# Row-tiled G matrices, a new split of the PSUM banks and a new order in a fused convolution and state-space kernel

## The chip, the cores and the metric

The kernel runs on one core of a Trainium2 chip. A core has five engines that work side by side, each through its own queue in order: TensorE (PE in the profile, its weight loads are PEld), VectorE (DVE), ScalarE (ACT), GpSimd (POOL) and SyncE (SP), which here issues the DMA transfers. The metric is the device time of one execution in microseconds. Three runs of the kernel before took 2834.29, 2833.24 and 2831.9 us, with a median of 2833.24 us. The profiled execution, from which all durations below come, took 2833.51 us and its trace spans 2831.8 us.

## What is computed

The input is 128 images of 128 channels and 16x16 pixels in float32. Layer 0 is a pair of quantised 3x3 convolutions with batch normalisation. Layer 1 reads each image as 256 tokens of 128 channels, runs a state-space mixer over the tokens forward and backward, and then a router with eight experts. The mixer is where the change lies. Cut to what matters, for each direction:

```
z, xbc, dt = split(x @ in_proj)
xbc  = silu(causal_conv4(xbc));  xh, B, C = split(xbc)     # 4 heads of 64; B and C have 64 rows
dt   = softplus(dt + dt_bias);   a = cumsum(dt * A)
L    = exp(a[l] - a[s]) for s <= l, else 0                 # per head
y[l] = sum_s (C[l] . B[s]) * L[l, s] * dt[s] * xh[s] + D * xh[l]
out  = rmsnorm(y * silu(z)) @ out_proj
```

The reference computes the sum over s in chunks of 64 tokens with a carried state. The kernel computes the same sum over an image's 256 tokens at once, in blocks of 128 by 128. The products C[l] . B[s] are the G matrices: one for each image and direction, with a contraction over only 64 rows.

## The kernel before

The first part of the kernel (up to about 297 us) is layer 0: statistics, the first convolution, the second. Layer 1 follows as a software pipeline over 64 steps. Step i handles two images (index k), that is 512 tokens, in two directions (index d). Its work is cut into parts, and each part is a Python generator whose pieces end at a `yield`:

- `a`: load, transpose, first layer norm. `c`: the dt chain, once for two steps, with small DVE pieces, and DMA transfers that bring the log decays into `rows` and `cols`.
- `x` (L747): input projections for xh, B and C: one matmul, one ACT pass and three DVE passes that read the PSUM bank (L762, L768). `bc` (L774): silu over B and C, and two DMA transfers that move C to the partitions where B lies. `sx`, `z`, `xt`: silu of xh, the gate z, the transpose of xh.
- `g` (L816): the G matrices, into PSUM. `s` (L828): exponents, bf16 matmuls, and the ACT exponential that empties the bank (L846). `m` (L849): DVE multiplies the exponentials by G (L852, L857) and so holds G's bank until then.
- `y` (L862): y = xh^T times the products. Here heads q=0 and q=1 use 64 output columns each, so two matmuls address two column halves of the array. `n`, `r`, `o`: norm and output projection.
- `e`, `p`, `f`: second layer norm, router, gates (with a DMA round trip through DRAM), GpSimd scaling (L1020), and the eight expert matmuls accumulated in one bank `f_ps` (L1032), which is copied out at L1035.

What sets the order is the table `T`. It gives each piece of each part a time in units of the pipeline's period. Piece n of step i gets the key i + T, all keys are sorted, and the pieces are issued in that order. So `T` fixes the order in every engine's queue, and nothing else: no instruction waits for its time, only for its operands and buffers.

In `part_g` before, one call handles one direction and one image. The stationary operand is the whole tile `bc` of that direction (128 partitions: B in one half, C in the other). The moving operand `cc` holds C in the rows that face B, and zeros in the other half. The zeros are written once, by four memsets at L584, ahead of the pipeline. The contraction so runs over 128 rows, of which 64 count.

PSUM has eight banks, which `BANKS` hands out by tag: x (projections, z, exponents) three, y two, f one, o (everything else, G too) two.

Of the kernel before, what the change touches and what calls it, by code (L numbers as in the profile page):

```python
# [8 lines left out]
F32 = mybir.dt.float32  # L9
# [5 lines left out]
P = 128  # L15
NT = 256
# [4 lines left out]
HD = 64  # L21
# [10 lines left out]
def kernel(ctx: ExitStack, tc: tile.TileContext, a: dict):  # L32
    from concourse import bass_isa

    nc = tc.nc
# [259 lines left out]
    with tc.tile_pool(name="w1p", bufs=1) as w1p:  # L295
# [15 lines left out]
        with tc.tile_pool(name="setup1", bufs=1) as setup, tc.tile_pool(  # L311
            name="psa", bufs=1, space=PSUM
# [8 lines left out]
            for i in range(NP):  # L321
                t = res.tile([P, 2, NT], F32, name=f"xr{i}", tag=f"xr{i}")
# [37 lines left out]
            for c in range(4):  # L360
                of = slice(cuts[c], cuts[c + 1])
# [33 lines left out]
                n = cuts[c + 1] - cuts[c]  # L395
# [145 lines left out]
    late = ctx.enter_context(tc.tile_pool(name="late", bufs=1))  # L541
# [34 lines left out]
                        )  # L576


    cczs = [[late.tile([P, 2 * NT], F32, name=f"cc{k}_{d}") for d in range(2)] for k in range(2)]
    gts = [late.tile([P, P], F32, name=f"gt{k}") for k in range(2)]  # L580
    daz = late.tile([P, 2, P], F32, name="daz")
    lwz = late.tile([P, P], F32, name="lwz")
    for t in (*cczs[0], *cczs[1], *gts, daz, lwz):
        nc.gpsimd.memset(t, 0.0)  # L584
    pr = ctx.enter_context(tc.tile_pool(name="pr", bufs=2))
    sm = ctx.enter_context(tc.tile_pool(name="sm", bufs=2))
    ps_ = ctx.enter_context(tc.tile_pool(name="ps", bufs=1, space=PSUM))
    BANKS = {"x": 3, "y": 2, "f": 1, "o": 2}

    def bank(name, tag):  # L590
        return ps_.tile([P, 512], F32, name=name, tag=tag, bufs=BANKS[tag])

# [8 lines left out]
    yts, uTs, xcs, xts, bcs, ccs, zs = {}, {}, {}, {}, {}, {}, {}  # L601
    gps, es, ygs, sqs, rrs, t2s, u2Ts, fps, gbs = {}, {}, {}, {}, {}, {}, {}, {}, {}
# [171 lines left out]
    def part_bc(i):  # L774

        bc = bcs[i]
        nc.scalar.activation(bc, bc, AF.Silu)
        yield

        cc = ccs[i] = cczs[i % 2]  # L780
        nc.sync.dma_start(cc[0][0:64, :], bc[64:128, 0, :])
        nc.sync.dma_start(cc[1][64:128, :], bc[0:64, 1, :])
        yield

    def part_sx(i, d):
# [27 lines left out]

    def part_g(i, d, k):  # L816

        tok = lambda s: slice(k * NT + s * P, k * NT + (s + 1) * P)
        g_ps = gps[i, d, k] = bank(f"g_ps{i}_{d}_{k}", "o")
        nc.tensor.matmul(  # L820
            g_ps[:, 0:NT], bcs[i][:, d, tok(d)], ccs[i][d][:, k * NT : (k + 1) * NT], start=True, stop=True
        )
        nc.tensor.matmul(  # L823
            g_ps[:, NT : NT + P], bcs[i][:, d, tok(1 - d)], ccs[i][d][:, tok(1 - d)], start=True, stop=True
        )
        yield

    def part_s(i, d, k, j):  # L828
# [193 lines left out]

    def part_f(i):

        f_ps = bank(f"f_ps{i}", "f")
        for t in range(4):
            nc.tensor.matmul(
                f_ps[:, t * P : (t + 1) * P], t2s[i][:, t, :], ident, start=(t == 0), stop=False, is_transpose=True
            )
        yield  # L1030
        for e in range(NE):
            nc.tensor.matmul(f_ps, ew[:, e, :], gbs[i, e], start=False, stop=(e == NE - 1))  # L1032
            yield
        ob = pr.tile([P, 2, NT], F32, name=f"ob{i}", tag="ob", bufs=1)
        nc.scalar.copy(ob.rearrange("p b s -> p (b s)"), f_ps)  # L1035
        yield
        nc.sync.dma_start(out_c[:, 2 * i : 2 * i + 2, :], ob)
        yield

    def part_t(i):  # L1040
# [4 lines left out]


    T = {
        ("a",): [0.0773, 0.0895, 0.1152, 0.2866, 0.3447, 0.4794, 0.4953, 0.5115],
        ("c",): [
            1.4709, 1.5225, 1.5731, 1.6594, 1.7098, 1.7751, 1.7801, 1.8040, 1.8079, 1.8309, 1.8542, 1.8594,  # L1050
            1.9139, 1.9270, 1.9323, 1.9709, 2.0549, 2.2383, 2.3648, 2.4555, 2.5636, 2.5771, 2.8047, 2.9326,
            2.9591, 3.1958, 3.3130, 3.3131, 4.1355, 4.1893,
        ],
        ("t",): [3.6635],
        ("x", 0, 2): [2.4693, 2.5057, 2.5934, 2.5972, 2.5984],
        ("x", 0, 0): [2.1661, 2.2763, 2.4457, 2.4862, 2.5014],
        ("x", 0, 1): [2.6018, 2.6937, 2.7181, 2.7588, 2.8003],
        ("x", 1, 2): [2.8997, 2.9367, 2.9373, 3.0152, 3.0293],
        ("x", 1, 0): [2.9802, 3.0015, 3.1146, 3.1362, 3.1518],
        ("x", 1, 1): [3.2863, 3.3092, 3.3641, 3.3704, 3.3905],  # L1060
        ("bc",): [3.4178, 3.4667],
        ("sx", 0): [2.9714],
        ("sx", 1): [3.5025],
        ("z", 0, 0): [3.2114, 3.2933],
        ("z", 0, 1): [3.4975, 3.5653],
        ("z", 1, 0): [3.3125, 3.4208],
        ("z", 1, 1): [3.5685, 3.5821],
        ("xt", 0, 0): [3.0438, 3.0552],
        ("xt", 0, 1): [3.3605, 3.4527],
        ("xt", 1, 0): [3.6676, 3.7471],  # L1070
        ("xt", 1, 1): [3.8466, 3.8846],
        ("g", 0, 0): [3.7660],
        ("s", 0, 0, 0): [3.6873, 3.7772],
        ("s", 0, 0, 1): [3.7508, 3.7854],
        ("s", 0, 0, 2): [3.8420, 3.8432],
        ("m", 0, 0): [3.8517, 3.8548],
        ("g", 0, 1): [3.9427],
        ("s", 0, 1, 0): [3.5860, 3.6728],
        ("s", 0, 1, 1): [3.8506, 3.9139],
        ("s", 0, 1, 2): [3.7919, 3.8284],  # L1080
        ("m", 0, 1): [3.9845, 3.9955],
        ("g", 1, 0): [4.0723],
        ("s", 1, 0, 0): [3.9718, 4.0401],
        ("s", 1, 0, 1): [4.0786, 4.1032],
        ("s", 1, 0, 2): [4.0576, 4.0790],
        ("m", 1, 0): [4.2309, 4.2498],
        ("g", 1, 1): [4.2898],
        ("s", 1, 1, 0): [3.6494, 3.7294],
        ("s", 1, 1, 1): [4.1026, 4.2262],
        ("s", 1, 1, 2): [3.9153, 3.9444],  # L1090
        ("m", 1, 1): [4.3058, 4.3095],
        ("y", 0, 0): [4.0126, 4.2204, 4.3180, 4.4089],
        ("y", 0, 1): [4.0291, 4.1343, 4.2948, 4.4250],
        ("y", 1, 0): [4.4415, 4.7048, 4.7862, 4.8156],
        ("y", 1, 1): [4.4007, 4.5565, 4.7642, 4.7846],
        ("n", 0): [4.7414, 4.7578, 4.8130],
        ("n", 1): [4.8600, 4.9321, 4.9637],
        ("r",): [4.9642],
        ("o", 0): [4.9857, 5.0427],
        ("o", 1): [4.9997, 5.0508],  # L1100
        ("e",): [
            5.0510, 5.2202, 5.2252, 5.2390, 5.2794, 5.2900, 5.3284, 5.3630, 5.3646, 5.3758, 5.3781, 5.3951,
            5.4117, 5.4132, 5.4233, 5.4552, 5.4561, 5.4691, 5.4826, 5.4906, 5.5973, 5.5985, 5.6126, 5.6739,
            5.6949, 5.6950, 5.7124, 5.7406, 5.7729,
        ],
        ("p", 0): [5.7845, 6.0128, 6.1273],
        ("p", 1): [6.0774, 6.1446, 6.2610],
        ("p", 2): [6.1581, 6.2483, 6.4846],
        ("f",): [6.0920, 6.1605, 6.2981, 6.5482, 6.5709, 6.6493, 6.7506, 6.8279, 6.9171, 7.0523, 7.5749],
        ("p", 3): [6.4896, 6.7491, 6.8564],  # L1110
    }
    parts = {
        "a": part_a, "c": part_c, "x": part_x, "bc": part_bc, "sx": part_sx, "z": part_z, "xt": part_xt, "g": part_g,
        "s": part_s, "m": part_m, "y": part_y, "n": part_n, "r": part_r, "o": part_o, "e": part_e, "p": part_p,
        "f": part_f, "t": part_t,
    }
    steps = []
# [41 lines left out]
```

## Time and profile before

| what | value |
|---|---|
| median of three runs | 2833.24 us |
| span of the trace | 2831.8 us |
| layer 0, up to the last convolution | about 297 us |
| two steady steps (1509.25 to 1585.85 us) | 76.60 us, so 38.30 us a step |
| PE busy in these 76.60 us | 76.31 us |
| DVE, ACT, POOL busy in them | 66.41, 62.82, 45.97 us |
| function table loads on ACT in them | 9, of 1283 ns each |
| granted PE clock in them | 1.00 |

The profile's page gives, in this order, the busy time of each engine, the same in 40 slices of the span, the DMA queues, the chain of work that ended last, and the costliest groups of instructions by source line. A float32 matmul stands in the trace as two instructions, a bf16 matmul or a transpose as one. [...]what a matmul costs in a stream is the distance from its start to the next one's start. The chain of waits shows these distances.

### The profile page before, as it was taken

The numbers are of one execution on the slowest core, as the hardware profiler recorded it, in microseconds if no ns is written. First come the engines' busy times: TensorE is split into PE (matmuls) and PEld (weight loads), VectorE is DVE, ScalarE is ACT, GpSimd is POOL, SyncE is SP. The second block draws the span as 40 slices with busy tenths as digits, with TensorE's granted clock in tenths as the row PEclk, the third lists the DMA queues.
The fourth block names the chain that finished last, engine by engine and source line by source line (L and its number), as shares of the span: only waits on it lengthen the run. The fifth ranks groups of instructions, "written<-read, shape, count | busy, mean of one in ns | idle before, by whom it ended". The sixth has DMA issues, their size and how long they took to land.

```text
span 2831.8 us, 48012 instructions
## 1 busy us (share of the span) xinstructions
PE 2640.0 (93%) x15830; PEld 1765.6 (62%) x15830; DVE 2387.6 (84%) x6315; ACT 2219.2 (78%) x3747; POOL 1592.5 (56%) x1619
## 2 busy tenths in 40 slices
PE   0687499999999999999999999999999999999997
PEld 0232256666667666666666666666666666666664
DVE  7799688888888888888888888888888888888883
ACT  5687498888888888888888888888888888888771
POOL 1353325656565665566565556556566666555666
PEclk9899799999999999999999999999999999999998
DMA  8259212232223233222223222322232222232232
GB/s 265 86 209 318 83 30 81 83 92 89 72 81 92 76 92 91 90 68 88 87 81 91 89 80 73 92 77 91 92 90 70 85 91 77 92 90 82 67 91 97
DMA packets 164553, 273.99 MB, mean 97 GB/s; under 512 B 46144, under 2 KB 89152, under 8 KB 164288
## 3 DMA queue, kind: packets, MB, share of 16 engines
q1 hardware_dynamic: 164288, 270.75, 31.0%
q8 instruction: 131, 2.15, 0.3%
q14 instruction: 134, 1.10, 0.1%
HBM read 196.66 MB, written 57.25 MB: 90 GB/s over the span
## 4 chain that ended last, share of the span: by engine, by line
PE 79%; ACT 9%; DVE 4%; issue 2%; DMA 1%; POOL 1%; SPq 0%; POOLq 0%; DVEq 0%; ACTq 0%
PE f_ps L1032 14%; PE x_ps L750 10%; PE y_ps L871 8%; PE o_ps L920 8%; PE z_ps L793 7%; PE xt_ps L805 4%; PE n_ps L900 4%; PE y_ps L877 4%; PE sg L836 4%; PE g_ps L820 3%; PE rt_ps L949 2%; PE dt_ps L660 2%; ACT u L621 2%; PE g_ps L823 1%; PE sg L838 1%
## 5 line engine op out<-in xcount | busy, mean ns | idle before, releaser
L1020 POOL TENSOR_TENSOR gb<-gb,u2T 128x512 f32<-128x512 f32 x512 | 645.6, 1277 | 9.6 <-DMA gb<-gd 8.6
L768 DVE SCALAR_TENSOR_TENSOR xc<-x_ps,cw,xc 128x510 f32<-128x510 f32 (+2 forms) x768 | 570.4, 743 | 60.0 <-ACT xc L762 51.6
L1032 PE MATMUL f_ps<-gb,ew 128*128 128x512 f32 x1024 | 526.3, 597 | 5.0 <-POOL gb L1020 4.8
L846 ACT ACTIVATE e<-sg 128x512 f32<-128x512 f32 x768 | 455.2, 594 | 49.9 <-PE sg L836 43.2
L887 POOL TENSOR_TENSOR yg<-yg,z 128x512 f32<-128x512 f32 x256 | 324.3, 1279 | 167.1 <-DVE yg L883 143.2
L852 DVE TENSOR_TENSOR e<-e,g_ps 128x1024 f32<-128x1024 f32 x256 | 311.9, 1218 | 113.9 <-PE g_ps L823 111.2
L750 PE MATMUL x_ps<-uT,wx 128*128 128x512 f32 x768 | 398.9, 601 | 2.9 <-ACT z L797 1.4
L809 ACT COPY xt<-xt_ps 128x512 f32<-128x512 f32 x256 | 149.2, 583 | 232.3 <-PE xt_ps L805 232.3
L871 PE MATMUL y_ps<-e,xt 128*64 128x256 f32 x2048 | 314.5, 385 | 0.3 <-DVE e L852 0.3
L768 DVE SCALAR_TENSOR_TENSOR bc<-x_ps,cw,bc 128x510 f32<-128x510 f32 (+2 forms) x384 | 284.7, 741 | 24.3 <-ACT bc L762 19.7
L793 PE MATMUL z_ps<-uT,wz 128*128 128x512 f32 x512 | 265.7, 602 | 2.0 <-ACT z L797 2.0
L920 PEld LDWEIGHTS o_ps<-wo,yg 128*128 128x128 f32 x2048 | 238.7, 192 | 29.9 <-issue 29.1
L990 POOL TENSOR_TENSOR e<-euler,e 128x4 f32<-128x4 f32 x64 | 66.1, 1032 | 335.3 <-DVE e L988 335.3
L1032 PEld LDWEIGHTS f_ps<-gb,ew 128*128 128x128 f32 x1024 | 176.2, 192 | 107.3 <-issue 86.5
L920 PE MATMUL o_ps<-wo,yg 128*128 128x128 f32 x2048 | 239.2, 275 | 0.1
L910 POOL TENSOR_TENSOR rr<-rr,mhalf 128x8 f32<-128x8 f32 x64 | 105.3, 1645 | 214.6 <-DVE rr L904 214.6
L896 POOL TENSOR_TENSOR sq<-sq,sq 128x512 f32<-128x512 f32 x128 | 163.3, 1276 | 109.3 <-ACT sq L890 109.2
L173 PE MATMUL cv<-hpad,wq 128*128 128x512 bf16 x640 | 164.1, 403 | 57.1 <-DVE hpad L165 54.1
L797 ACT ACTIVATE z<-z_ps 128x512 f32<-128x512 f32 x256 | 152.6, 597 | 81.2 <-PE z_ps L793 79.1
L762 ACT ACTIVATE xc<-x_ps,cb,cw 128x512 f32<-128x512 f32 x256 | 198.0, 773 | 13.3 <-PE x_ps L750 9.1
L877 PE MATMUL y_ps<-e,xt 128*64 128x128 f32 x2048 | 198.9, 273 | 0.0
L836 PE MATMUL sg<-rows,cols 128*128 128x256 bf16 x1024 | 195.3, 273 | 1.0 <-ACT e L846 0.8
(247 smaller groups left out, 5712.8 us busy)
## 6 DMA issues: line engine op xcount, KB each, us to landing
gb<-gd SPq DMA_DIRECT2D x256, 512.0 KB
xr<-in_x SPq DMA_DIRECT2D x64, 256.0 KB
y<-xr SPq DMA_DIRECT2D x64, 256.0 KB
y<-y SPq DMA_DIRECT2D x64, 256.0 KB
cc<-bc SPq DMA_DIRECT2D x128, 128.0 KB
out<-ob SPq DMA_DIRECT2D x64, 256.0 KB
o<-o SPq DMA_DIRECT2D x56, 256.0 KB
q<-o SPq DMA_DIRECT2D x56, 256.0 KB
```

Source lines behind the costliest of these rows:

```text
L750: nc.tensor.matmul(ps, wx[d][:, n * P : (n + 1) * P], uTs[i], start=True, stop=True)
L768: nc.vector.scalar_tensor_tensor(acc[:, :, to], raw[:, :, of], cw[:, d, n, 3 - back : 4 - back], acc[:, :, to], ALU.mult, ALU.add,)
L793: nc.tensor.matmul(ps, wz[:, d, n * P : (n + 1) * P], uTs[i], start=True, stop=True)
L836: nc.tensor.matmul(sg[:, :, of], c_[:, k, d, s, half, :], r_[:, :, d, t, of], start=True, stop=True)
L846: nc.scalar.activation(e0[:, :, t, :] if j < 2 else e1, sg, AF.Exp)
L852: nc.vector.tensor_tensor(e0.rearrange("p h t l -> p h (t l)"), e0.rearrange("p h t l -> p h (t l)"), gps[i, d, k][:, 0:NT].unsqueeze(1).t ...
L871: nc.tensor.matmul(y_ps[64 * q : 64 * q + 64, k, :], xt[:, 2 * k + s0, 64 * h : 64 * h + 64], e0[:, h].rearrange("p t l -> p (t l)"), star ...
L877: nc.tensor.matmul(y_ps[64 * q : 64 * q + 64, k, s1 * P : (s1 + 1) * P], xt[:, 2 * k + s1, 64 * h : 64 * h + 64], e1[:, h, :], start=False ...
L887: nc.gpsimd.tensor_tensor(yg, yg, zs[i, d][:, n, :], ALU.mult)
L920: nc.tensor.matmul(o_ps[:, (2 * j + d) * P : (2 * j + d + 1) * P], ygs[i, d, n][:, t * P : (t + 1) * P], wo[d][:, n, :], start=(n == 0), s ...
L1020: nc.gpsimd.tensor_tensor(gb[:, e], gb[:, e], u2Ts[i], ALU.mult)
L1032: nc.tensor.matmul(f_ps, ew[:, e, :], gbs[i, e], start=False, stop=(e == NE - 1))
```

## The change

Four things change.

1. `cc` becomes one tile from a rotating pool. Forward C goes to partitions 0 to 63, backward C to partitions 64 to 127. There is no zero half, and the four memsets go.
2. `part_g` now handles both directions of one image. Each matmul contracts over 64 rows only. Forward uses the upper 64 rows of the array and backward the lower 64, in adjacent pairs: first the two 128x256 blocks, then the two 128x128 blocks. The two directions write two different banks.
3. `BANKS`: x has two banks instead of three, y keeps two but also serves `f_ps`, and o has four instead of two.
4. `T` is replaced as a whole. Each part keeps its pieces; their order in each queue changes.

```
-    cczs = [[late.tile([P, 2 * NT], F32, name=f"cc{k}_{d}") for d in range(2)] for k in range(2)]
...
-    for t in (*cczs[0], *cczs[1], *gts, daz, lwz):
+    for t in (*gts, daz, lwz):
         nc.gpsimd.memset(t, 0.0)
...
-    BANKS = {"x": 3, "y": 2, "f": 1, "o": 2}
+    BANKS = {"x": 2, "y": 2, "o": 4}
...
-        cc = ccs[i] = cczs[i % 2]
-        nc.sync.dma_start(cc[0][0:64, :], bc[64:128, 0, :])
-        nc.sync.dma_start(cc[1][64:128, :], bc[0:64, 1, :])
+        cc = ccs[i] = pr.tile([P, 2 * NT], F32, name=f"cc{i}", tag="cc")
+        nc.sync.dma_start(cc[0:64, :], bc[64:128, 0, :])
+        nc.sync.dma_start(cc[64:128, :], bc[0:64, 1, :])
...
-    def part_g(i, d, k):
+    def part_g(i, k):
+        g_ps = [bank(f"g_ps{i}_{d}_{k}", "o") for d in range(2)]
         tok = lambda s: slice(k * NT + s * P, k * NT + (s + 1) * P)
-        g_ps = gps[i, d, k] = bank(f"g_ps{i}_{d}_{k}", "o")
-        nc.tensor.matmul(
-            g_ps[:, 0:NT], bcs[i][:, d, tok(d)], ccs[i][d][:, k * NT : (k + 1) * NT], start=True, stop=True
-        )
-        nc.tensor.matmul(
-            g_ps[:, NT : NT + P], bcs[i][:, d, tok(1 - d)], ccs[i][d][:, tok(1 - d)], start=True, stop=True
-        )
+        for s, to, of in ((0, slice(0, NT), slice(k * NT, (k + 1) * NT)), (1, slice(NT, NT + P), None)):
+            for d in range(2):
+                rows_ = slice(HD * d, HD * d + HD)
+                t = tok(d) if s == 0 else tok(1 - d)
+                nc.tensor.matmul(
+                    g_ps[d][:, to], bcs[i][rows_, d, t], ccs[i][rows_, t if of is None else of], start=True, stop=True
+                )
...
-        f_ps = bank(f"f_ps{i}", "f")
+        f_ps = bank(f"f_ps{i}", "y")
...
-        ("g", 0, 0): [3.7660],
-        ("s", 0, 0, 0): [3.6873, 3.7772],
+        ("g", 0): [4.8439],
+        ("s", 0, 0, 0): [4.7381, 4.7593],
...
-        ("y", 1, 0): [4.4415, 4.7048, 4.7862, 4.8156],
-        ("y", 1, 1): [4.4007, 4.5565, 4.7642, 4.7846],
+        ("y", 1, 0): [5.4960, 5.5576, 5.7044, 5.8186],
+        ("y", 1, 1): [5.3862, 5.4334, 5.7041, 5.8037],
...
-        ("f",): [6.0920, 6.1605, 6.2981, 6.5482, 6.5709, 6.6493, 6.7506, 6.8279, 6.9171, 7.0523, 7.5749],
+        ("f",): [7.3274, 7.3434, 7.4166, 7.7003, 7.8571, 7.9726, 8.0377, 8.1134, 8.1688, 8.1967, 8.3291],
```

## The prediction, made before the changed kernel had run

> **What bounds the kernel now.** I read the page first: the busy shares of the engines and the same in slices.
>
> ```profile
> PE 2640.0 (93%) x15830; PEld 1765.6 (62%) x15830; DVE 2387.6 (84%) x6315; ACT 2219.2 (78%) x3747; POOL 1592.5 (56%) x1619
> ...
> PE   0687499999999999999999999999999999999997
> ```
>
> From slice 6 to the last but one PE is never below 90%. Then I cut two steady steps out of the middle, at the starts of two output projections, and asked for the busy time of each half.
>
> ```profile
> 1509.25:1547.50 38.25, 37.96 (x233) 25.91 (x233) 32.62 (x87) 31.79 (x52) 22.81 (x23) 1.00 0.27 82
> 1547.50:1585.85 38.35, 38.35 (x244) 26.93 (x243) 33.79 (x92) 31.04 (x53) 23.16 (x23) 1.00 0.28 85
> ```
>
> The columns are window, length, then busy time of PE, PEld, DVE, ACT, POOL. PE fills the 38.30 us of a step; DVE needs 33.2, ACT 31.4, POOL 23.0. So a step costs what PE's queue costs, and the other engines count only where PE waits for them. The chain of waits in these windows shows what each piece costs on PE, start to start:
>
> ```profile
> 1512.82 0.58 PE y_ps L871 x4
> 1513.40 0.22 PE y_ps L877 x4
> 1513.62 0.43 PE y_ps L871 x4
> ...
> 1515.57 0.60 PE xt_ps L805 x4
> ...
> 1520.40 1.28 ACT L698
> ...
> 1522.62 0.49 ACT u2T L945
> 1523.11 0.04 issue
> 1523.16 1.16 PE rt_ps L949 x8
> ...
> 1537.77 0.44 PE xt_ps L805 x4
> ...
> 1540.50 0.43 PE g_ps L820 x2
> 1540.94 0.22 PE g_ps L823 x2
> ```
>
> The reader is to see three things. One float32 matmul of 256 columns (two instructions) costs 0.43 us in G. In y, two of them (x4) cost the same 0.43 us, so the two column halves run at once. The first group of a y visit costs 0.58 instead of 0.43 us, and the transposes after it 0.60 instead of 0.44: entering and leaving the tiled mode costs 0.15 + 0.16 = 0.31 us. And once in two steps the chain leaves PE for 7 us of ACT work with a table load of 1.28 us (L698) in it.
>
> **What the Trainium skill says.** "TensorEngine Tiling (Array Packing)", Key Properties: changing the tiling mode drains TensorE; the tiles load weights and multiply independently. The trace agrees for column halves (0.31 us a visit, two matmuls in the time of one); it has no row tiles. The same page, Gotcha 1: different row tiles must write different PSUM banks, as the change has it. "TensorE: Matmul & The Clock Gate", Measured speedup vs the span model: four row tiles gave 3.07x, three column tiles 2.38x, about 77 to 79% of the ideal; y here reaches all of its 2x. "ScalarE: Activation LUTs", What ACT_TABLE_LOAD costs: about 1283 ns and a drain of about 1380 ns; the trace shows 1283 ns and the next ACT instruction at once, so I use 1.28 us.
>
> **The change part by part**, per step, on PE.
>
> G. Before: 4 calls x (0.43 + 0.22) = 2.60 us. After: 2 calls, each two pairs. With y's overlap a pair costs one matmul, so 2 x 0.65 = 1.30: a saving of 1.30 us. Bounds: 0 (no overlap) and 1.30. If only the weight loads went one after the other, a 128x256 pair would stay at 0.43 and a 128x128 pair cost 0.43 (four loads of 0.11), so 2 x 0.86 = 1.72 and a saving of 0.88. I take 1.30: y's two halves start within 0.01 us of each other, weight loads included.
>
> Mode changes. Before there are two y visits a step, each with both heads' calls (n = 0 and 1) side by side. In the new order y(0,1) and y(0,0) stand side by side, but y(1,1) and y(1,0) are parted by f, z and x matmuls, because f now holds one of the two y banks over 0.87 of a period (keys 7.3274 to 8.1968). So there are three y visits and two G visits: 3 more, 3 x 0.31 = +0.93 us.
>
> ACT's table loads. In ACT's order the changed kernel has 129 in the pipeline against 286: the Silu pieces now stand together, and so do the exponentials. (286 - 129) x 1.283 / 64 = 3.1 us a step less, so ACT falls from 31.4 to 28.3 us. ACT is not the bound; what counts is PE's wait. In the two steps above the half with the r matmuls (1.06 + 0.44 = 1.50 us) has 0.29 us less of PE work than the half with the dt matmuls (2 x 0.89), yet from one output projection to the next it takes 1547.67 - 1509.25 = 38.42 against 38.18 us. The stall is 0.53 us in two steps, 0.26 a step. The load at L698 is in its chain and goes: -0.26. Bounds: 0 and -0.36, which adds the small delays of the z and x matmuls.
>
> Banks. With two x banks an exponent matmul waits for the exponential two places ahead. A handover costs 0.16 (a sg matmul shows 0.38 but its successor starts after 0.22) + 0.59 (L846) + two semaphores of some 0.03 = 0.81 us. The PE work in between, in the new order: before s(0,0,2) one x, 0.86; before s(1,1,0) two transposes, 0.88; before s(1,1,2) gt and f, 0.97; before x(1,2) n and s, 1.11. In the old order the shortest was 1.08. Before s(0,0,2) ACT also does exponential, transpose copy, exponential: 0.16 + 0.59 + 0.58 + 0.59 + 0.09 = 2.01 us against 1.97 of PE work. So these places are just met or missed by hundredths: +0.10 us, bounds 0 and 1.25 (five places late by 0.25 each). DVE's banks have more room: x(0,1) to s(0,0,1) has 4.14 us of PE work against 0.16 + 0.77 + 3 x 0.74 + 0.1 = 3.25. The single y bank is free 0.16 + 0.74 after y(1,1); x, f and z, 2.58 us, stand in between. G holds its o banks until m, for which there are now four.
>
> DMA. `cc` still takes two transfers of 128 KB. On SP they stand behind the fourth gb load, which waits for f's second expert (key 7.4166). That is 0.43 of a period, some 16 us, before G, and the longest late transfer on the chain took 3.98 us. Other transfers move with their parts and keep over 5 us. I cost these at nothing: PE's own queue hides them.
>
> Sum per step: -1.30 + 0.93 - 0.26 + 0.10 = -0.53 us. PE is the bound from about 385 to 2766 us, 62 steps: -33 us.
>
> The start. Four memsets go from the head of POOL's queue:
>
> ```profile
> 298.90 8.42 POOL L584 MEMSET cc<- 128x512 f32 x4 [64.28 <-DMA parts<-none]
> ...
> 306.78 2.15 DVE L565 CAST cols<-triple 128x3072 bf16<-128x3072 f32 x1
> ...
> 309.74 8.67 POOL L572 TENSOR_SCALAR_AFFINE_SELECT cols<-far 64x256 bf16<-64x256 bf16 x24
> 318.38 1.02 POOL L616 TENSOR_TENSOR rstda<-rstda,mhalf 128x4 f32<-128x4 f32 x1
> ```
>
> The first layer norm's power on POOL at 318.38 is on the chain, and everything on POOL ahead of it stands in a row. Without the 8.42 us the selects start earlier, but the last third of them needs DVE's cast that ends at 308.93: 308.93 + 8.67/3 = 311.8. So 318.4 - 311.8 = -6.6 us.
>
> Fill and drain. From the first x to the last piece the keys span 7.57 - 2.17 = 5.41 periods before and 8.33 - 3.34 = 4.99 after; the prefetch that makes the pipeline look longer is only an earlier load. The tail after the last output projection (2794.4 to the end, 37 us) is the same chain of router, DMA and experts. The fill loses one or two table loads from its chain: -1 us, between -5 and +4.
>
> Together -33 - 6.6 - 1 = -40.6 us. The profiled span, 2831.8, lies 1.4 below the median of the three runs, which agree within 0.1%; I put the difference on the median: 2833.2 - 40.6 = about 2793 us.
>
> **The rivals.**
> - Weight loads in series: saving 0.88 instead of 1.30, 0.42 x 62 = 26 us less, so 2819. For it: 128 weight columns for each row tile against 64 in y, and 77% in the skill's four-tile figure. Against it: the two row tiles' loads fill different rows, and together no more of the array than one full load.
> - No overlap, the change doing only harm on PE: +1.30 x 62 = 81, so 2873. Against it: y.
> - Slower by the x banks: all five tight handovers late by 0.25 us. Price 1.25 instead of 0.10, so 2793 + 71 = 2864. It decides from 0.10 + 40.6/62 = 0.75 us a step, 0.15 at each place. For it: ACT's queue is in order, and one late copy delays the exponentials behind it. Against it: ACT now idles a quarter of the step, so a delay is caught up before the next group.
> - Better: G visits drain for half the price and no handover misses: -0.10 - 0.30 = -0.40 x 62 = -25, so 2768.
>
> **How the numbers follow.** Likeliest 0.62 (2778 to 2812 by itself: fill and drain, 0 to 0.36 of stall, 0 to 0.3 of new waits); weight loads in series 0.15; better 0.10; x banks 0.08; no overlap 0.05. Time 2793. For 8 in 10 the range takes in the likeliest, the series case and half of the better one: 2768 to 2828. About 0.2% is what a measurement of this kernel can tell from no change: 2827.6 to 2838.9. Faster gets the likeliest, the better and nearly all of the series case, 0.86; the two slow cases give 0.11 for slower; 0.03 remains.
>
> **What would show it.** G's lines: pairs starting within 0.02 us, 0.43 and 0.22 us a pair, some 0.15 us more at each end of a visit. Five tiled visits a step. ACT near 28.3 us a step with two table loads. A step of 37.8 us in the windows. The power at L616 near 312. Wrong would be: pairs in series, PE gaps before s(0,0,2), s(1,1,0) or s(1,1,2) of over 0.15 us each, or a step of over 38.2 us.

## The result, and the profile after

The changed kernel took 2848.61 us (median of four runs, 2846.3 to 2856.03), the kernel before 2833.76 us (median of four runs). The ratio is 1.0057, with a 95% interval of 1.0036 to 1.0077: slower by 0.6%. The profiled execution is the slowest of the four (2856.03, span 2854.3), so the sums below, made against its span, exceed the median difference of 14.9 us.

The page of the changed kernel: busy shares, PE in slices, and the chain of work that ended last by engine.

```profile
PE 2639.9 (92%) x15830; PEld 1681.4 (59%) x15830; DVE 2377.6 (83%) x6315; ACT 2036.2 (71%) x3590; POOL 1593.8 (56%) x1615
...
PE   0687489999999999999999999999999999999997
...
PE 72%; DVE 8%; DMA 6%; ACT 3%; POOL 3%; issue 2%; SPq 1%; POOLq 0%; DVEq 0%; ACTq 0%
```

PE is as busy as before, to 0.1 us, although two of the G matmuls now run at once. That equality misleads: a matmul's shown time runs on past the start of the next (0.59 us for one of 512 columns, whose starts lie 0.43 us apart), so it can cover part of a wait. In the first experiment below, where the waits are gone, the same matmuls are busy for 2618.1 us. PE's share of the chain fell from 79% to 72%, and DMA's rose from 1% to 6%: something that PE did not wait for before is now on the path. Two neighbouring steps, cut at the starts of two output projections (the columns are those of the prediction's windows):

```profile
1489.21:1527.13 37.92, 37.92 (x244) 25.20 (x242) 31.78 (x92) 28.51 (x50) 23.04 (x23) 1.00 0.26 85
1527.13:1565.93 38.80, 38.15 (x236) 24.92 (x234) 34.67 (x87) 28.51 (x49) 23.13 (x23) 1.00 0.28 84
```

One step takes about the predicted time, the next is longer and PE has gaps in it. ACT is down to 28.5 us, about as predicted (28.3). Over the 54 steps from the fifth output projection on, the steps alternate between a mean of 37.70 and one of 39.56 us, 38.63 together; before they took 38.30. The chain through one step (start, length, what):

```profile
1983.01 0.85 PE g_ps L823 x8
1983.86 1.05 PE f_ps L1034 x2
...
1991.15 0.85 PE g_ps L823 x8
1992.00 0.32 PE sg L838 x2
...
2016.32 0.04 issue
2016.36 4.54 DMA cc<-bc
2020.90 0.04 issue
2020.95 1.29 PE g_ps L823 x7
```

A visit is one stay of PE in a tiled mode. The first two G visits are what the change is for: eight instructions, four matmuls of two directions, in 0.85 us where the two calls of before took 1.30. The last one waits for a transfer of `cc` that landed at 2020.9. SP's queue (SPq; start, length, line) says why that one was late:

```profile
1972.22 0.34 SPq L1018 DMA_DIRECT2D gb<-gd  x1
1972.61 0.54 SPq L780 DMA_DIRECT2D cc<-bc  x1
1973.24 0.54 SPq L781 DMA_DIRECT2D cc<-bc  x1
...
2013.02 2.66 SPq L727 DMA_DIRECT2D parts<-part  x4
2015.78 0.54 SPq L1018 DMA_DIRECT2D gb<-gd  x1
2016.36 0.51 SPq L780 DMA_DIRECT2D cc<-bc  x1
2016.92 0.59 SPq L781 DMA_DIRECT2D cc<-bc  x1
```

In the first step `cc` is issued 10 us before its G. In the other step SP first waits for part `c`'s last cast on DVE (until 2013.0), issues its four `parts` transfers, then the gb load, and only then `cc`: 3.3 us later, and another 4.5 us until it has landed. The part `c` runs once in two steps; that is why every second step is long. Over the whole trace PE waited 29 times for `cc` (total, times, longest):

```profile
PE g_ps L823 <- DMA cc<-bc: 29.6, 29, 2.3
```

The 29.6 us are only the part that shows as a wait for the transfer. The stretch from the first to the second output projection of a step is a better measure. It is 7.07 us in every steady step without `parts`. In those with `parts` it is 8.75 us on average, and between 7.42 and 11.33.

### The profile page after: what moved, and what is told of

Its sections match the earlier page's. It is cut to its first block, busy times and chain, and to the rows that moved or that the text cites. A ratio compares the mean times of both kernels' runs of the same rounds, so it can differ in the third digit from the quotient of the medians.

```text
span 2854.3 us, 47377 instructions
## 1 busy us (share of the span) xinstructions
PE 2639.9 (92%) x15830; PEld 1681.4 (59%) x15830; DVE 2377.6 (83%) x6315; ACT 2036.2 (71%) x3590; POOL 1593.8 (56%) x1615
## 4 chain that ended last, share of the span: by engine, by line
PE 72%; DVE 8%; DMA 6%; ACT 3%; POOL 3%; issue 2%; SPq 1%; POOLq 0%; DVEq 0%; ACTq 0%
PE f_ps L1034 14%; PE x_ps L749 10%; PE y_ps L873 7%; PE z_ps L792 7%; PE o_ps L922 5%; DMA cc<-bc 5%; PE g_ps L823 4%; PE sg L838 4%; PE y_ps L879 3%; PE xt_ps L804 3%; PE n_ps L902 3%; PE dt_ps L659 2%; PE rt_ps L951 2%; PE cv L173 1%; PE sg L840 1%
## 5 line engine op out<-in xcount | busy, mean ns | idle before, releaser
L1034 PE MATMUL f_ps<-gb,ew 128*128 128x512 f32 x1024 | 534.9, 605 | 2.7 <-POOL gb L1022 1.8
L749 PE MATMUL x_ps<-uT,wx 128*128 128x512 f32 x768 | 408.9, 614 | 6.6 <-DVE xc L767 3.3
L922 PE MATMUL o_ps<-wo,yg 128*128 128x128 f32 x2048 | 249.8, 275 | 0.0
L885 DVE SCALAR_TENSOR_TENSOR yg<-xc,dcol,y_ps 128x512 f32<-128x512 f32 x256 | 189.2, 739 | 23.9 <-PE y_ps L879 23.8
L873 PEld LDWEIGHTS y_ps<-e,xt 128*64 128x64 f32 x2048 | 117.3, 136 | 147.0 <-issue 95.5
L879 PEld LDWEIGHTS y_ps<-e,xt 128*64 128x64 f32 x2048 | 147.0, 137 | 74.0
```

Source lines behind the costliest of these rows:

```text
L749: nc.tensor.matmul(ps, wx[d][:, n * P : (n + 1) * P], uTs[i], start=True, stop=True)
L873: nc.tensor.matmul(y_ps[64 * q : 64 * q + 64, k, :], xt[:, 2 * k + s0, 64 * h : 64 * h + 64], e0[:, h].rearrange("p t l -> p (t l)"), star ...
L879: nc.tensor.matmul(y_ps[64 * q : 64 * q + 64, k, s1 * P : (s1 + 1) * P], xt[:, 2 * k + s1, 64 * h : 64 * h + 64], e1[:, h, :], start=False ...
L922: nc.tensor.matmul(o_ps[:, (2 * j + d) * P : (2 * j + d + 1) * P], ygs[i, d, n][:, t * P : (t + 1) * P], wo[d][:, n, :], start=(n == 0), s ...
```

## The experiments

**Is `cc` late only because of what stands ahead of it?** One key of `T` is moved:

```
-        ("bc",): [4.1463, 4.8377],
+        ("bc",): [4.1463, 4.7300],
```

> The changed kernel with one key moved: the two transfers that fill cc go to SP's queue at 0.73 of a period instead of 0.84, ahead of the four transfers to parts (0.7333) and of the fourth gb load. Theory A (cc is late only because it stands behind the four parts transfers of part c on SP, in one step of two): the wait of G for cc goes, the stretch from the first to the second output projection of the step with parts falls from a mean of 8.75 to about 7.1 us, two steps take some 75.5 us instead of 77.2, and 32 pairs save about 54 us: about 2795 us. Rival B (PE would be stopped there anyway, by the two x banks or by DVE's queue, and the wait for cc only covers it): the wait moves to another releaser and the time stays above 2835 us.

Measured: 2806.05 us (2805.31 to 2806.16), 0.9898 of the kernel before (0.9883 to 0.9913). The stretch is 7.07 us in every steady step, and no wait of G for `cc` is left.

```profile
1538.07:1575.99 37.92, 37.92 (x243) 25.20 (x241) 32.16 (x92) 28.52 (x50) 23.05 (x23) 1.00 0.27 85
1575.99:1613.48 37.49, 37.49 (x235) 24.65 (x233) 33.69 (x87) 28.31 (x49) 23.05 (x23) 1.00 0.28 87
```

PE fills both steps without a gap. SP's queue in the second one:

```profile
1586.81 0.54 SPq L780 DMA_DIRECT2D cc<-bc  x1
1587.44 0.54 SPq L781 DMA_DIRECT2D cc<-bc  x1
1601.09 2.61 SPq L727 DMA_DIRECT2D parts<-part  x4
```

`cc` now goes out 14 us ahead of `parts`, in time that SP had idle. One number in a table turned 0.6% slower into 1.0% faster. The gain is 42.6 us on the medians and 49.9 on the profiled spans; the 54 expected had been read from the slowest run of the changed kernel. The four runs of the changed kernel spread over 9.7 us, those of this one over 0.9, so the lateness probably varied from run to run too; only one of the four was profiled.

**The same from the other side:** `cc` keeps its place, and the four `parts` transfers go behind it.

```
-            3.5521, 3.7333, 4.3290, 4.4984, 4.7686, 5.0091,
+            3.5521, 3.8380, 4.3290, 4.4984, 4.7686, 5.0091,
```

> The changed kernel with the other key moved: the four parts transfers go behind cc (0.8380 instead of 0.7333), cc keeps its key, and the fourth gb load stays ahead of cc. Theory A: the parts transfers alone are what delays cc, so this does the same as moving cc: about 2795 us, within 5 us of it. Rival C (cc's own key, a quarter of a microsecond of plan ahead of G, or the gb load ahead of it is the cause): the wait of G for cc stays in both steps and the time stays above 2820 us.

Measured: 2805.25 us (2803.81 to 2808.36), the same as with `cc` early. So neither `cc`'s own key nor the gb load ahead of it was the cause. It was the four `parts` transfers, with the wait for DVE's cast that they bring into SP's queue. How much of it is the wait and how much the issuing (2.7 us in the step shown) was not taken apart.

**What do the row tiles give?** In the kernel with `cc` early, G goes back to 128 rows with zeros in half of them, in the same places of the plan:

```
-                    g_ps[d][:, to], bcs[i][rows_, d, t], ccs[i][rows_, t if of is None else of], start=True, stop=True
+                    g_ps[d][:, to], bcs[i][:, d, t], ccs[i][d][:, t if of is None else of], start=True, stop=True
```

> As the kernel with cc early, but G's matmuls run over all 128 rows again with the zero halves of before (two cc tiles of each parity, the four memsets back), in the same places and in the same plan. Theory (a row-tiled pair takes the time of one matmul and a visit costs 0.31 us): two pairs of calls cost 2.60 instead of 1.30 + 2 x 0.31 = 1.92 us, so +0.68 us a step, 63 steps: +43 us against the kernel with cc early, about 2838 us. Rival (the mode changes eat the overlap, or PE isn't the bound there): less than 10 us more than the kernel with cc early.

Measured: 2840.52 us (2839.84 to 2844.63), 34.5 us more than with `cc` early; a step takes 38.36 instead of 37.76 us, so 0.60 us. Its chain shows the G calls of both directions in the old form, with no cost behind them:

```profile
1587.56 1.31 PE g_ps L823 x8
1588.87 0.86 PE f_ps L1034 x2
```

Row-tiled, the same pair of lines is 0.85 and 1.05. The tiles save 0.46 inside and lose 0.19 behind (0.10 where an exponent matmul follows), so 0.27 to 0.36 us a visit. Without the row tiles the new plan, `cc` mended, is 0.3% slower than the kernel before (1.0026, 1.0014 to 1.0037). So without the tiles nothing of the gain is left: a step of 38.36 us is no shorter than the 38.30 of before. By the terms worked out below, the third y visit (some 0.34 us) takes what the table loads bring (0.36).

**What was the table load at L698 worth?** In the kernel before, the table for Exp ahead of exponential (1,0,0) is replaced by the one that holds Exp and Ln:

```
-        nc.scalar.preload_act_table_set("natural_log_exp_and_others")
-        yield
+        for _ in range(2):
+            nc.scalar.preload_act_table_set("natural_log_exp_and_others")
+            yield
...
-        ("t",): [3.6635],
+        ("t",): [3.6635, 4.0390],
```

> The kernel before with a table load that holds both Exp and Ln put in the place of the Exp load ahead of exponential (1,0,0): the load at L698 goes, 30 loads in all, nothing else changes. Theory of the prediction (the load at L698 is a stall of 0.53 us in two steps): the step of 38.42 us falls to about 37.9, 30 pairs save 16 us: about 2818 us. Rival (PE has other work there, or the chain through layer norm and transposes waits for something else): within 5 us of the kernel before.

Measured: 2811.04 us (2809.51 to 2813.83), 0.9914 (0.9901 to 0.9928). That is 23 us from thirty table loads, in the old plan. In the same comparison the whole change with `cc` early brings 28 us (2834.14 to 2806.05), so one load fewer in two steps is worth most of what all four changes together bring.

```profile
1500.08:1537.78 37.70, 37.70 (x234) 26.06 (x233) 32.70 (x87) 30.64 (x52) 22.96 (x23) 1.00 0.28 82
1537.78:1575.96 38.18, 38.18 (x243) 26.77 (x242) 33.62 (x92) 30.89 (x53) 22.96 (x23) 1.00 0.31 85
```

The step of 38.18 is untouched, the one of 38.42 falls to 37.70: a stall of 0.72 us in two steps, 0.36 a step.

**Why did the start not get shorter?** First the selects (L572) of POOL were put behind the first two layer norms of the pipeline, in the kernel with `cc` early:

```
         yield from layernorm(yt, u, f"a{i}")
+        if i == 1:
+            selects()
```

> The kernel with cc early, with the 24 selects on POOL (L572) put behind the first two layer norms of the pipeline instead of ahead of them; DVE's and ACT's casts and the memsets stay where they are. Theory (in the start the chain goes through the selects, and they can't start before DVE's casts are done, whatever else is taken from POOL's head): the first power at L615 comes at about 310 instead of 317.7 us, and the whole kernel ends about 7.5 us earlier: about 2798.5 us against about 2806. Rival (something else, such as the casts or part c, sets the start): no change within 3 us.

Measured: 2801.26 us (2796.38 to 2801.66), 4.8 us less than with `cc` early in the medians. The first power came 10.2 us after the first cast instead of 17.8, the whole 7.5 us; but another DVE instruction gave 3.2 us back:

```profile
319.83 8.70 POOL L575 TENSOR_SCALAR_AFFINE_SELECT cols<-far 64x256 bf16<-64x256 bf16 x24
...
325.17 3.44 DVE L676 SCALAR_TENSOR_TENSOR ex<-dtr 128x64 f32<-128x64 f32 x1
```

This instruction takes 0.23 us elsewhere. It ended 0.1 us after the last select. All 24 selects stood in one row there, and ten of them ended while it waited; the expectation that follows has 13, which are only those from 323.8 us on. So the selects were split, 13 behind the first layer norm and 11 behind the second.

> The kernel with cc early and the selects late, the selects now in two parts: 13 behind the first layer norm (into 5 us in which POOL and DVE wait), 11 behind the second. Theory (the first exponent's input on DVE, L676, took 3.44 instead of 0.23 us because 13 selects in a row on POOL kept DVE from its second operand): that instruction is back at about 0.25 us, and the kernel ends 3.2 us earlier than with the selects in one piece, about 2798 us. Rival (another step of the start sets the end): no change from 2801 us.

Measured: 2796.21 us (2795.15 to 2796.88), 0.987 of the kernel before (0.9853 to 0.9886). That is 5.0 us less than with the selects in one piece, though one of the four runs of that version took 2796.38, and 1.7 us of it is an earlier end of layer 0 in the profiled run. From DVE's first cast to the fifth output projection it is 2.8 us less, near the 3.2 expected. The same instruction:

```profile
323.45 0.23 DVE L678 SCALAR_TENSOR_TENSOR ex<-dtr 128x64 f32<-128x64 f32 x1
```

The other direction, POOL behind DVE's casts, was asked by putting the memsets behind the selects. In the first attempt the order on POOL hardly changed: the memsets still ran ahead of the selects, so it tells nothing of the question.

> The kernel with cc early, with the four memsets that are left moved from ahead of the selects on POOL to behind them. Theory of the prediction (POOL's queue is the limit: the first two thirds of the selects need only casts that are done by 304 us): the selects begin near 303 us, the last third follows DVE's last cast, and they are done by about 312.5 us. Rival (POOL stands still for as long as DVE's casts run): whatever stands at the head of POOL's queue, the selects are not done before about 317 us.

Measured: 2802.4 us (2801.41 to 2803.4, two runs), 3.6 us less than with `cc` early for nearly the same order. A difference of that size between two of these versions says little by itself. The split selects, measured together with this run, are 6.2 us faster than it.

The second attempt put them behind the first layer norm:

```
         yield from layernorm(yt, u, f"a{i}")
+        if i == 0:
+            for t in (*gts, daz, lwz):
+                nc.gpsimd.memset(t, 0.0)
```

> The kernel with cc early, with the four memsets that are left moved behind the first layer norm, so that the selects stand at the head of POOL's queue (in the run before, the scheduler had left the memsets ahead of them). Theory of the prediction (POOL's queue is the limit): the selects begin near 303 us, behind the first cast, the last eight follow DVE's last cast at about 309.5 us, and the first power comes at about 312.5 us. Rival (POOL stands still for as long as DVE's casts run): the selects are not done before about 317 us, and the power stays near 318 us.

Measured: 2802.25 us (two runs).

```profile
300.79 14.81 POOL L572 TENSOR_SCALAR_AFFINE_SELECT cols<-far 64x256 bf16<-64x256 bf16 x24
302.23 3.91 DVE L561 CAST rows<-ident 64x2048 bf16<-64x2048 f32 x3
306.06 1.74 DVE L565 CAST cols<-triple 128x3072 bf16<-128x3072 f32 x1
...
315.57 1.02 POOL L613 TENSOR_TENSOR rstda<-rstda,mhalf 128x4 f32<-128x4 f32 x1
```

The selects now stand first and start at 300.8, but the first three took 1.80, 1.37 and 4.19 us, up to the end of DVE's casts at 307.8. Then the other 21 came 0.36 us apart, even those of the first tile, whose cast had been done before the first select began. The first three ended 0.26 to 0.28 us after the end of one of DVE's casts each. The casts in this run began 1.8 us earlier than with `cc` early; measured from them, the power came 1.1 us earlier, where the prediction's theory had some 6. So POOL all but stands still while DVE casts.

**The drain.** With `cc` early the kernel still needs 48.3 us from the first output projection of the last step to the end; before it was 41.1. In the router of the last step small DVE operations are slow (the changed kernel):

```profile
2827.67 4.95 POOL L1022 TENSOR_TENSOR gb<-gb,u2T 128x512 f32<-128x512 f32 x4
2827.73 1.23 DVE L994 TENSOR_SCALAR g<-e 128x4 f32<-128x4 f32 x1 [1.15 <-POOL e L992]
```

In the kernel before the same operation of the last step took 0.17 us, with no gb multiplication on POOL beside it. The experiment moved the multiplications and expert matmuls of the last step but one by 0.6 of a period:

> The kernel with cc early; for the last step but one alone, the multiplications of gb on POOL and the expert matmuls are moved 0.6 of a period later, behind the router of the last step. Theory (in the drain the small DVE operations of the router take 1.2 instead of 0.2 us where they stand beside a gb multiplication on POOL, some 4 us in all, and the last power waits behind multiplications on POOL): the router of the last step gets its 4 to 5 us back, the multiplications move into the wait for the transfers behind it, and the kernel ends 3 to 5 us earlier, about 2802 us against 2806. Rival (the drain is set by the sum of POOL's multiplications): no change, or up to 5 us later.

Measured: 2816.08 us (2814.6 to 2820.06), 10 us more than with `cc` early. Neither part came true. Three multiplications still started right behind the router's power, so L994 again took 1.23 us; and the chain then went three times through a gb load (3.6, 6.0 and 4.1 us), since the loads wait for the three gb buffers, which the expert matmuls now released late (SP waited four times for them, 13.8 us in all). What the drain would take without the contention stays open.

**A bank for f again**, taken from o, so that y(1,1) and y(1,0) can stand side by side:

```
-    BANKS = {"x": 2, "y": 2, "o": 4}
+    BANKS = {"x": 2, "y": 2, "f": 1, "o": 3}
...
-        ("y", 1, 0): [5.4960, 5.5576, 5.7044, 5.8186],
+        ("y", 1, 0): [5.3863, 5.4800, 5.7044, 5.8186],
```

> The kernel with cc early, but f has a bank of its own again, taken from o (x 2, y 2, f 1, o 3), and y(1,0) stands right behind y(1,1): four tiled visits a step instead of five. Theory (a visit costs 0.15 in and 0.15 to 0.20 us out, and PE's queue is the bound): 0.32 us a step less, 62 steps: -20 us, about 2786 us. Rival (with three banks for o, G's pair leaves one for transposes, n and o, and PE waits for copies): no gain, 2806 us or more.

Measured: 3117.61 us (3116.68 to 3121.53), a step of 42.7 us. Two of PE's waits there, between 700 and 2600 us:

```profile
PE yt_ps L632 <- DVE e L859: 42.3, 22, 1.9
...
PE g_ps L823 <- ACT xt L808: 24.2, 45, 0.5
```

L859 is the multiplication that frees G's bank, L808 the copy that frees a transpose's. With G's pair in two of three banks, everything else in o passes through one. These waits are not the whole of the loss, as PE also waited for ACT behind an x bank (30.9 us in the same stretch), and the run moved keys of y too; what each is worth was not taken apart. In this order, then, three o banks don't suffice for the row-tiled pairs, and the fourth is taken from f, which parts the y visits.

## Why the prediction was wrong

The forecast was 2793 us and faster; it became 2848.6 and slower. The step that failed is **DMA, costed at nothing**. It says that on SP `cc` stands "behind the fourth gb load, which waits for f's second expert", 16 us before G. That is SP's order only as far as the predecessor that was looked at. In the sorted keys, `parts` (3.7333, so 0.7333 within a period) stands ahead of that gb load (7.7717) and of `cc` (4.8377), and it waits for DVE's last cast. The figure of 16 us was the age of one dependency, not the time at which the queue is free. "Other transfers move with their parts and keep over 5 us" passed over just the transfers that mattered, and none of the rivals had the DMA queue in it. Measured, the price is (8.75 - 7.07)/2 = 0.84 us a step in the profiled run, so that a step changed by +0.33 us instead of -0.53 (by the medians, 42.6 us in 62 steps, it is 0.69). Taking away this queueing alone, from either side, gives 2805 to 2806 us. The 13 us still missing to 2793 lie in the start and the drain. Of the prediction's signs of being wrong, the step of over 38.2 us is the one that came.

The other steps, each against its term:

- *The sum per step.* Forecast 37.77 us; with `cc` early the steps take 37.92 and 37.60, so 37.76. That it agrees so closely is partly luck: three terms were off by 0.04 to 0.10 us and cancel.
- *G.* The pairs do overlap (their two matmuls start within 0.01 us of each other), -1.30 us: the rivals "weight loads in series" and "no overlap" fall. The Trainium skill, "TensorEngine Tiling (Array Packing)", Key Properties, has tiles that load weights and multiply independently; the trace agrees for row tiles too (0.85 us with the entry, against 1.31 for the four full matmuls).
- *Mode changes.* Five visits, as forecast. A visit costs 0.15 (y) to 0.20 (G) us at its start and 0.10 to 0.20 behind it, depending on what follows: 0.69 for the two G visits and some 0.34 for the third y visit, so +1.03 instead of +0.93. The row-tile experiment agrees: 1.30 - 0.69 = 0.61, measured 0.60.
- *Table loads.* Mechanism right, size off: -0.36 in the old plan instead of -0.26, the far end of the bounds. The PE work of the two half steps had been summed from r and dt alone (0.29 us apart); in the experiment they differ by 38.18 - 37.70 = 0.48.
- *Banks.* +0.10 forecast. The one handover that shows with `cc` early is an exponent matmul behind four transposes, late by some 0.24 us in 12 of 27 steps with `parts`: these take 37.60 us on average and 37.49 at best, so (37.60 - 37.49)/2, about +0.06 a step. The x-bank rival falls. The place is not one of those that the forecast named, and the holder of the bank not an exponential of ACT: in the late steps looked at, DVE's last pass over B and C in that bank ended 0.21 us before the matmul started (770.84 and 771.05 us in the first). DVE's banks were the ones said to have more room.
- *The start.* -6.6 forecast; the first power came at 317.69 instead of 318.38, while layer 0 happened to end 1.1 us later; counted from DVE's first cast that is -1.8. What was left out is that POOL and DVE held each other up. The kernel before, then the one after:

```profile
309.42 0.20 POOL L584 MEMSET lwz<- 128x128 f32 x1
```

```profile
303.37 3.75 DVE L561 CAST rows<-ident 64x2048 bf16<-64x2048 f32 x3
...
304.87 4.07 POOL L583 MEMSET lwz<- 128x128 f32 x1
...
309.05 8.66 POOL L572 TENSOR_SCALAR_AFFINE_SELECT cols<-far 64x256 bf16<-64x256 bf16 x24
```

  The same memset takes 0.20 us alone and 4.07 us beside casts. So the 8.42 us of the four removed memsets, which stood beside the same casts, were not their own price, and what stands behind them waits for the casts with or without them.
- *Fill and drain.* -1 forecast, within -5 to +4. The drain costs more: 46.4 us from the last step's first output projection to the end against 41.1. Of these 5.3 us, four DVE operations beside gb multiplications (L994, L998, L1002, L1004) make up 3.9, with 4.62 us against 0.71 before.

For the profiled runs this closes: start and fill to the fifth output projection +0.1 us, 55 steps at +0.34 = +18.8, the next four steps -1.7, drain +5.3: +22.5 us, the difference of the spans. With `cc` early the same four are -2.2, -29.3, -3.1 and +7.2: -27.4 us, against -40.6 in the forecast.

## What to carry to other kernels

When an order is changed, list for each transfer everything that now stands ahead of it in its queue, with what each of those waits for, and not just its nearest predecessor; here four transfers behind one late cast cost more than a new tiling brought. A busy queue's time is set by the latest dependency in it, so early, ready transfers belong ahead of late ones. If a change is slower and its own lines look as hoped for, look for one piece that waits at every second period, and move only that.

## What the hardware showed that was not expected

POOL and DVE hold each other up, which their queues don't show. While DVE cast float32 to bf16, three POOL selects took 1.37 to 4.19 us instead of 0.36, and a memset 4.07 instead of 0.20. While POOL ran 24 selects without a pause, one DVE operation with two operands in SBUF took 3.44 instead of 0.23 us: it waited not for one select but until the last was done. Beside gb multiplications small DVE operations took up to 1.24 instead of 0.17 to 0.19 us. The Trainium skill, "Trainium Architecture — The Big Picture", What this means for kernel authors, says that DVE and GpSimd share a port pair under an exclusive lock; these durations agree with it, though no run here tests the ports themselves. The late and split selects show what an order on one queue is worth: counted from DVE's first cast, the fifth output projection came 7.5 us earlier in the profiled run than with `cc` early (241.4 against 248.9).

The fastest version measured, the change with `cc` early and the selects split, takes 2796.21 us: 1.3% less than the kernel before, and 1.8% less than the changed one.
